# Depthwise taps on 32x32 tiles of TensorE: the two lanes interleaved tile by tile, in the order of columns

## The chip, the cores and the metric

The kernel runs on one NeuronCore of a Trainium2 chip. The metric is the device time of one execution in microseconds (us), and a kernel is judged by the median of its runs. TensorE (PE) multiplies and writes sums to PSUM; VectorE (DVE) and ScalarE (ACT) read PSUM and work on SBUF; GpSimd (POOL) and SyncE (SP) do little here but start DMAs.

## The reference, cut to what matters

The program is a net of four layers, x = x + layer(group_norm(x)), on x of 4 x 48 x 256 x 256 in f32. Layers 0 and 3 are feed-forward blocks with a spectral weight and a depthwise 3x3 convolution; layers 1 and 2 are line-by-line recurrences. Only layer 3 is touched by the change:

```python
y = jnp.einsum('oc,bchw->bohw', w_in, x)             # 48 -> 288 channels
f = jnp.fft.rfft2(yp) * fft_mask[None]               # in patches of 8 x 8
yp = jnp.fft.irfft2(f, s=(P, P))
...
y = lax.conv_general_dilated(y, w_dw, (1, 1), ((1, 1), (1, 1)), feature_group_count=C2)   # 3 x 3, per channel
x1, x2 = jnp.split(y, 2, axis=1)                     # 144 and 144 channels
g = jax.nn.gelu(x1, approximate=False) * x2
return jnp.einsum('oc,bchw->bohw', w_out, g)         # 144 -> 48
```

The depthwise convolution is nine taps: each output pixel is the sum over nine shifted input pixels of that channel, each times one weight.

## The kernel before

Layer 3 goes over the images in pairs. Each pair is cut into strips of eight rows, and one more short "tail" strip at the end of each pair, so there are 2 x 33 steps. In each step the strip is normalised (`normed`), turned and carried to the spectral basis (`turned`, `waves`, L1006 and L1021), multiplied by w_in and the mask (`spectrum`, `spectrum_rest`, L1040 to L1056) and carried back to pixels (`pixels`, `pixels_rest`, L1087 to L1113). The pixels stand in five tiles `zt`: a0 and a1 (the first 128 channels of x1 and of x2, first image), b0 and b1 (the same of the second image), and m (the 16 channels that are left, of both images).

**The taps.** A depthwise tap is a matmul with a diagonal 32 x 32 weight (`diag`): 32 channels (a block k of 32 partitions, a row block of the array) go to 32 partitions of PSUM (a column block j of the array). A matmul covers two image rows, 512 pixels; j counts the four pairs of rows of a strip. So block k and pair j name one of the sixteen 32 x 32 tiles of the array. `taps` (L1117) does a0, a1 and m in this way. `lower_taps` (L1130) does the lower half of the strip for b0 and b1, with the four column blocks made of two halves x two pairs of rows. The upper half of b is done by VectorE (`begin`, L1172, with L1183), one tap at a time from the list `due`.

**The two lanes.** A unit (`unit`, L1248) is one tile of PSUM sums, `pd`, of two banks: lane 0 has blocks 0 and 1, lane 1 has blocks 2 and 3. When its nine taps are done, the unit ends with the evacuation: `curve` (ScalarE Gelu, L1160), `gate` (VectorE product, L1166), or `lower_gate` (ScalarE L1149, then VectorE L1150). `together` (L1272) runs one unit of each lane side by side and is called a round here. A generator gives a whole tap of its lane at each step, so TensorE's queue holds, tap after tap, the eight matmuls of lane 0 and then the eight of lane 1. Within a lane the order is: for each column block, its two row blocks. Because m takes four blocks for both images, the lists of units are staggered: over two steps there are seven rounds, in which lane 0 does a0, a1, b, m, a0, a1, b and lane 1 does a0, a1, b, a0, a1, b, m.

**What sets the order.** On TensorE, VectorE and ScalarE the order is written out by hand (`manual_schedule`). The loop over steps (L1338) puts the spectral work of the next step and the pixels of this one between the rounds, and `store` (with `mixed`, L1197 to L1237) multiplies the last step's gated values by w_out, adds the input and writes the rows out. All sums of TensorE in layer 3 share one ring of four PSUM buffers (`ps_w`, tag "w"), each of two banks: a new tile waits until the tile four places before it has been evacuated. So the lane 0 `pd` of a round waits for one earlier tile and the lane 1 `pd` for the next one; the first two tiles after a round take the two other buffers, and the third one takes the buffer of lane 0.

Of the kernel before, what the change touches and what calls it, by code (L numbers as in the profile page):

```python
# [31 lines left out]
class Net:  # L32
# [848 lines left out]
    def layer3(self, x, scs):  # L881
# [9 lines left out]
        tail = lambda step: step[1] == H // RB  # L891
        odd = lambda step: steps.index(step) % 2
        with ExitStack() as st:
# [222 lines left out]

            def taps(step, g, half, blocks, pd):  # L1117
                for t in range(9):
                    for j in range(1 if tail(step) else 4):
                        n = 1 if tail(step) else R2  # L1120
                        for i, k in enumerate(blocks):
                            s = slice(32 * k, 32 * k + 32)
                            nc.tensor.matmul(  # L1123
                                pd[32 * j : 32 * j + 32, i, 0:n, :], diag[s, 2 if g == "m" else half, t, :],
                                zt[g][s, R2 * j + t // 3 : R2 * j + t // 3 + n, t % 3 : t % 3 + W],
                                start=(t == 0), stop=(t == 8),
                            )
                    yield True

            def lower_taps(step, blocks, pd):  # L1130


                for t in range(9):
                    for half in range(2):
                        for j in range(2, 4):
                            to = slice(64 * half + 32 * (j - 2), 64 * half + 32 * (j - 1))
                            for i, k in enumerate(blocks):
                                s = slice(32 * k, 32 * k + 32)
                                nc.tensor.matmul(  # L1139
                                    pd[to, i], diag[s, half, t, :],  # L1140
                                    zt[f"b{half}"][s, R2 * j + t // 3 : R2 * j + t // 3 + R2, t % 3 : t % 3 + W],
                                    start=(t == 0), stop=(t == 8),
                                )
                    yield True

            def lower_gate(k0, pd):
                gl = io.tile([128, 2, MM], F32, name="gl", tag="gl")
# [100 lines left out]
            def unit(l, step, img):  # L1248


                n, blocks = steps.index(step), (2 * l, 2 * l + 1)
                pd = None
                if img == "b":
                    if not tail(step):
                        pd = ps_w.tile([128, 2, R2, W], F32, name="pd", tag="w")
                        yield from lower_taps(step, blocks, pd)
                else:
                    pd = ps_w.tile([128, 2, R2, W], F32, name="pd", tag="w")
                    half = int(img[1]) if img[0] == "a" else 0
                    yield from taps(step, img, half, blocks, pd)  # L1260
                if img == "a0":
                    waiting[l] = curve(step, pd)
                    return
                assert n == 0 or steps[n - 1] in out
                if img == "a1":
                    gate(step, "a", 2 * l, waiting[l], pd)
                elif img == "m":
                    gate(step, img, 0, curve(step, pd[:, 0:1]), pd[:, 1:2])
                elif pd is not None:
                    lower_gate(2 * l, pd)  # L1270

            def together(k, aside=None):  # L1272


                going = [unit(l, *units[l][k]) for l in range(2)]
                for t in range(9):
                    for g in list(going):
                        if next(g, None) is None:
                            going.remove(g)
                    if t == 1 and aside is not None:  # L1280
                        aside()
                    if due and (t + 1) * 5 // 9 > t * 5 // 9:
                        due.pop(0)[1]()
                for g in going:
                    assert next(g, None) is None
# [51 lines left out]
            k = 0  # L1337
            for n, step in enumerate(steps):  # L1338
# [6 lines left out]
                if even:  # L1345
                    turn(n + 1, "AD")
                together(k, None if even else lambda: ready(n + 1))

                pixels(step, "a1", "DD")
# [6 lines left out]
                else:  # L1356
                    turn(n + 1, "AA")
                together(k + 1)

                upper(n, 1, "AA")  # L1360
# [3 lines left out]
                else:  # L1364
                    wave(n + 1, "AA")
                    spectra(n + 1, 0, slice(0, 2))
                together(k + 2)
                k += 3
                if not even:
# [118 lines left out]
```

## Time and profile before

| what | value |
|---|---|
| median of 3 runs | 13252.56 us (13247.61 to 13270.56) |
| the profiled execution, its own time | 13259.28 us |
| its span, first to last instruction | 13257.5 us |
| mean granted TensorE clock | 0.966 |
| layer 3's taps, first to the end of the program | 8690 to 13257 us |
| TensorE busy in the span | 12356.8 us (93%) |
| matmuls L1123 into sums from z_a, from z_m; L1139 | 37152, 9288; 18432 records |

How to read it: times in the profile are in us, those of single instructions in ns. PE is TensorE's matmuls and PEld its weight loads. A line of groups gives the source line, engine, operation, the tiles out<-in with their shapes, the number of instructions, then busy time and the mean time of one, and then the idle time of the engine just before them with what ended it. A line in order of time gives the start, the length from the first start to the last end, and the number of instructions that were merged into it; square brackets hold idle time and its releaser. Matmuls overlap on the array, so the length of one is much more than its share of the time.

### The profile page before, as it was taken

The page shows a single profiled execution, that of the slowest core. Times are in us where ns is not written, and L with a number is a line of the kernel's source. Part 1 is how long each engine was busy: PE and PEld are TensorE (multiplying, and loading weights), DVE is VectorE, ACT ScalarE, POOL GpSimd, SP SyncE. Part 2 cuts the span into 40 slices and gives each one's busy share as a digit, 9 for nine tenths or more (in the row PEclk, how much of TensorE's full clock was granted, in tenths as well). Part 3 has the DMA queues.
Part 4 walks back from the last instruction along what each step waited for, and adds up shares of the span by engine and source line. Part 5 has one row for each costly group of instructions (what it writes and reads, how often), then busy time and mean ns, then how long its engine had stood idle before and what let it go on. Part 6 is the DMA issues. An engine that isn't in the chain of part 4 may idle for free.

```text
span 13257.5 us, 432328 instructions
## 1 busy us (share of the span) xinstructions
PE 12356.8 (93%) x203336; PEld 8155.9 (62%) x203336; DVE 7417.3 (56%) x10766; ACT 3602.9 (27%) x4043; POOL 1336.7 (10%) x977
## 2 busy tenths in 40 slices
PE   2999999998999899999998999989999999999999
PEld 1333333335777677767776777666666666666666
DVE  6777777773333334653333336556666666666666
ACT  1444444442223100002232000033333333333333
POOL 0011011010000002530000015400000000000000
PEclk9999999998999999999999999889999999999999
DMA  7222222225755876987657769711111111111110
GB/s 171 59 55 57 55 57 59 52 54 101 153 134 153 172 153 147 229 177 152 136 153 165 157 135 220 179 31 27 23 27 27 24 27 23 27 27 23 27 27 20
DMA packets 1170374, 1225.00 MB, mean 92 GB/s; under 512 B 1027669, under 2 KB 1031757, under 8 KB 1107725
## 3 DMA queue, kind: packets, MB, share of 16 engines
q1 hardware_dynamic: 1070476, 649.55, 25.6%
q0 software_dynamic: 87488, 445.55, 11.6%
q10 hardware_dynamic: 10624, 102.24, 4.4%
q8 instruction: 1592, 26.08, 0.9%
q14 instruction: 194, 1.58, 0.0%
HBM read 699.76 MB, written 497.42 MB: 90 GB/s over the span
## 4 chain that ended last, share of the span: by engine, by line
PE 88%; ACT 4%; issue 3%; DVE 3%; DMA 2%; SPq 0%; POOL 0%; DVEq 0%; ACTq 0%; POOLq 0%
PE acc L661 40%; PE pd L1123 12%; PE pd L308 9%; PE pd L1139 5%; PE pz L1040 4%; PE pp L1087 4%; PE po L1215 2%; PE ph L285 2%; PE pz L1053 2%; DMA gx<-in_x 1%; PE ph L277 1%; PE py L382 1%; PE po L452 1%; PE py L389 1%; PE po L1205 1%
## 5 line engine op out<-in xcount | busy, mean ns | idle before, releaser
L661 PE MATMUL acc<-line,w_down 96*96 96x256 f32 x12240 | 2692.9, 382 | 53.0 <-ACT line L731 31.8
L661 PEld LDWEIGHTS acc<-line,w_down 96*96 96x96 f32 x12240 | 2008.1, 164 | 730.1 <-DVE line L740 34.1
L1123 PE MATMUL pd<-z_a,diag 32*32 32x512 f32 x37152 | 1626.2, 599 | 57.8 <-issue 49.4
L308 PE MATMUL pd<-main,diag 32*32 32x512 f32 x36864 | 1427.2, 621 | 81.4 <-issue 77.3
L661 PE MATMUL acc<-line,w_right 96*96 96x256 f32 x6120 | 1341.0, 380 | 81.8 <-DVE line L811 59.8
L661 PE MATMUL acc<-line,w_left 96*96 96x256 f32 x6120 | 1362.9, 384 | 31.2 <-DVE line L852 31.2
L1183 DVE SCALAR_TENSOR_TENSOR acc<-z_b,wd,acc 128x1024 f32<-128x1024 f32 (+1 forms) x1056 | 1326.5, 1259 | 34.4 <-ACT acc L1178 7.1
L345 DVE SCALAR_TENSOR_TENSOR acc<-rest,wd,acc 128x1024 f32<-128x1024 f32 x1024 | 1257.8, 1292 | 126.9 <-ACT acc L339 126.6
L1123 PEld LDWEIGHTS pd<-z_a,diag 32*32 32x32 f32 x37152 | 890.6, 103 | 604.0 <-issue 232.9
L661 PEld LDWEIGHTS acc<-line,w_right 96*96 96x96 f32 x6120 | 1000.1, 164 | 412.6 <-DVE line L811 61.1
L661 PEld LDWEIGHTS acc<-line,w_left 96*96 96x96 f32 x6120 | 1007.9, 165 | 377.5 <-DVE line L852 47.1
L308 PEld LDWEIGHTS pd<-main,diag 32*32 32x32 f32 x36864 | 505.2, 105 | 798.1 <-issue 684.4
L1139 PE MATMUL pd<-z_b,diag 32*32 32x512 f32 x18432 | 973.7, 642 | 0.5 <-ACT z_b L999 0.5
L740 DVE TENSOR_TENSOR line<-acc,in 96x256 f32<-96x256 f32 x1020 | 428.9, 421 | 961.6 <-PE acc L661 948.7
L814 DVE SCALAR_TENSOR_TENSOR line<-acc,b_right,in 96x256 f32<-96x256 f32 x1020 | 489.4, 480 | 836.4 <-PE acc L661 836.4
L775 DVE SCALAR_TENSOR_TENSOR line<-acc,b_down,in 96x256 f32<-96x256 f32 x992 | 475.9, 480 | 811.5 <-PE acc L661 810.6
L120 ACT ACTIVATE nrm<-nrm 96x2 f32<-96x2 f32 (+2 forms) x5 | 1.0, 204 | 2989.4 <-DVE nrm L119 2989.4
L852 DVE SCALAR_TENSOR_TENSOR line<-acc,b_left,in 96x256 f32<-96x256 f32 x992 | 475.8, 480 | 564.2 <-PE acc L661 564.2
L862 POOL TENSOR_TENSOR blk<-blk,line 96x1024 f32<-96x1024 f32 x248 | 705.2, 2873 | 644.3 <-DVE line L852 644.3
L1043 DVE TENSOR_TENSOR z<-pz,mask 128x1024 f32<-128x1024 f32 x512 | 601.2, 1219 | 276.2 <-PE pz L1040 273.7
L782 ACT COPY blk<-line 96x1024 f32<-96x1024 f32 (+2 forms) x264 | 480.0, 1891 | 978.0 <-DVE line L775 816.0
L1087 PEld LDWEIGHTS pp<-c_inv,z 64*64 64x64 f32 x32768 | 515.9, 135 | 228.8 <-issue 204.6
(167 smaller groups left out, 13065.8 us busy)
## 6 DMA issues: line engine op xcount, KB each, us to landing
blk<-x ACTq DMA_DIRECT2D x64, 1536.0 KB, 19.3
in<-x SPq DMA_DIRECT2D x248, 384.0 KB, 11.0
dn<-line POOLq DMA_DIRECT2D x124, 768.0 KB, 9.6
rt<-line POOLq DMA_DIRECT2D x124, 768.0 KB, 9.6
in<-rt SPq DMA_DIRECT2D x124, 768.0 KB, 12.6
in<-dn SPq DMA_DIRECT2D x120, 768.0 KB, 5.8
in<-up SPq DMA_DIRECT2D x240, 384.0 KB, 9.3
up<-blk POOLq DMA_DIRECT2D x56, 1536.0 KB, 14.3
```

The lines of the kernel that those rows point to most:

```text
L308: nc.tensor.matmul(pd[32 * j : 32 * j + 32, i], diag[s, t, :], z[s, R2 * j + t // 3 : R2 * j + t // 3 + R2, t % 3 : t % 3 + W], start=(t = ...
L345: nc.vector.scalar_tensor_tensor(to, at(t, r), wd[:, 1, t : t + 1], to, ALU.mult, ALU.add)
L661: self.nc.tensor.matmul(acc, w[:, t, :], carry[:, :, t : t + m], start=(t == 0), stop=(t == 2))
L782: nc.scalar.copy(blk[:, :, e, lo:hi, k // 2 : k // 2 + RH], inner(ln[:, e::2])[..., lo:hi].rearrange("p h i w -> p i w h"),)
L814: nc.vector.scalar_tensor_tensor(blocks(inner(line)), blocks(acc), br, new, ALU.add, ALU.add)
L862: (nc.vector if w0 == 0 else nc.gpsimd).tensor_tensor(part, part, inner(ln[:, f::2])[..., lo:hi].rearrange("p w i h -> p i h w"), ALU.add)
L1040: nc.tensor.matmul(pz[:, b, q, :], xf[s, q0 + q, :], wi[s, NM * k : NM * k + NM], start=True, stop=True)
L1043: nc.vector.tensor_tensor(zs[k][:, q0 : q0 + 4].rearrange("p q b c -> p b q c"), pz, mask[:, :, :, NM * k : NM * k + NM].to_broadcast([128 ...
L1087: nc.tensor.matmul(pp[64 * c : 64 * c + 64, l, q, :], z[f, q0 + q, b, 64 * c : 64 * c + 64], self.inv1[f, :], start=True, stop=True,)
L1123: nc.tensor.matmul(pd[32 * j : 32 * j + 32, i, 0:n, :], diag[s, 2 if g == "m" else half, t, :], zt[g][s, R2 * j + t // 3 : R2 * j + t // 3 ...
L1139: nc.tensor.matmul(pd[to, i], diag[s, half, t, :], zt[f"b{half}"][s, R2 * j + t // 3 : R2 * j + t // 3 + R2, t % 3 : t % 3 + W], start=(t ...
L1183: nc.vector.scalar_tensor_tensor(acc, at(t), wd[:, half, t : t + 1], acc, ALU.mult, ALU.add)
```

## The change

In `taps` the generator now stops after each column block j, not after each tap: it has given two matmuls (one for each of the lane's two row blocks). In `lower_taps` it stops after each pair of matmuls too. `together` steps both lanes four times per tap. TensorE's queue so holds, in each tap: column block 0 of lane 0 (row blocks 0 and 1), column block 0 of lane 1 (row blocks 2 and 3), column block 1 of lane 0, and so on: the sixteen tiles in the order of columns. In a tail step only column block 0 has work, and the other three stops are empty. What happens once per tap beside it (`aside` at t == 1, a VectorE tap from `due`) stays where it was. The weights, the sums, the buffers and their number, and the instructions of the other engines are the same.

```diff
             def taps(step, g, half, blocks, pd):
                 for t in range(9):
-                    for j in range(1 if tail(step) else 4):
+                    for j in range(4):
                         n = 1 if tail(step) else R2
-                        for i, k in enumerate(blocks):
+                        for i, k in enumerate(blocks) if j == 0 or not tail(step) else ():
                             s = slice(32 * k, 32 * k + 32)
                             nc.tensor.matmul(
                                 pd[32 * j : 32 * j + 32, i, 0:n, :], diag[s, 2 if g == "m" else half, t, :],
                                 zt[g][s, R2 * j + t // 3 : R2 * j + t // 3 + n, t % 3 : t % 3 + W],
                                 start=(t == 0), stop=(t == 8),
                             )
-                    yield True
+                        yield True
...
             def lower_taps(step, blocks, pd):
...
                                     start=(t == 0), stop=(t == 8),
                                 )
-                    yield True
+                            yield True
...
                 going = [unit(l, *units[l][k]) for l in range(2)]
                 for t in range(9):
-                    for g in list(going):
-                        if next(g, None) is None:
-                            going.remove(g)
+                    for _ in range(4):
+                        for g in list(going):
+                            if next(g, None) is None:
+                                going.remove(g)
                     if t == 1 and aside is not None:
                         aside()
```

## The prediction

> **What bounds the kernel now.** I read the page first, then the windows of the stage that the change touches, then single rounds of it in order of time.
>
> ```profile
> span 13257.5 us, 432328 instructions
> PE 12356.8 (93%) x203336; PEld 8155.9 (62%) x203336; DVE 7417.3 (56%) x10766; ACT 3602.9 (27%) x4043; POOL 1336.7 (10%) x977
> ...
> PE 88%; ACT 4%; issue 3%; DVE 3%; DMA 2%; SPq 0%; POOL 0%; DVEq 0%; ACTq 0%; POOLq 0%
> PE acc L661 40%; PE pd L1123 12%; PE pd L308 9%; PE pd L1139 5%; PE pz L1040 4%; PE pp L1087 4%; PE po L1215 2%; PE ph L285 2%; PE pz L1053 2%; DMA gx<-in_x 1%; PE ph L277 1%; PE py L382 1%; PE po L452 1%; PE py L389 1%; PE po L1205 1%
> ...
> L1123 PE MATMUL pd<-z_a,diag 32*32 32x512 f32 x37152 | 1626.2, 599 | 57.8 <-issue 49.4
> L1139 PE MATMUL pd<-z_b,diag 32*32 32x512 f32 x18432 | 973.7, 642 | 0.5 <-ACT z_b L999 0.5
> ```
>
> TensorE is the path, and the lines that change (L1123, L1139) hold 17% of it, all in layer 3. From the first L1123 to the end:
>
> ```profile
> 8690.00:13257.00 4567.00, 4376.90 (x127017) 3056.65 (x127014) 2934.61 (x3068) 1589.31 (x2325) 5.69 (x15) 0.97 0.12 25
> ```
>
> TensorE is busy 4376.9 of 4567.0 us. Every f32 matmul of the program is two records, a first and a second pass, each with its weight load: 288 records for the 9 x 16 matmuls of a round. So a gain has to come from a denser round, and a loss from a round that starts or ends later. One round, lane 0 under L1123 and lane 1 under L1139:
>
> ```profile
> 10495.76 0.66 PE L1123 MATMUL pd<-z_a,diag 32*32 32x512 f32 x8
> 10495.81 0.66 PE L1139 MATMUL pd<-z_b,diag 32*32 32x512 f32 x8
> 10496.21 0.63 PE L1123 MATMUL pd<-z_a,diag 32*32 32x512 f32 x8
> 10496.27 0.63 PE L1139 MATMUL pd<-z_b,diag 32*32 32x512 f32 x8
> 10496.64 0.90 PE L1123 MATMUL pd<-z_a,diag 32*32 32x512 f32 x8
> 10496.95 0.72 PE L1139 MATMUL pd<-z_b,diag 32*32 32x512 f32 x8
> ```
>
> All sixteen first passes begin within 0.1 us, then all sixteen second passes: already in the old order sixteen tiles run at once. The first tap takes 0.857 us (two passes of 0.429). The second starts at 10496.64 with one matmul alone; the next weight load comes at 10496.831. That is 0.031 us after the first matmul's second pass has ended (10496.213, and 0.587 long). In a round at half clock the same load comes at 8729.318, where that pass began at 8728.231 and took 1.056: again 0.031. So the load of matmul n+17 waits until matmul n has wholly ended. Later taps confirm 17, not 16: the stalled load moves one matmul earlier in each tap, through both lanes and all columns. A matmul's turn is 0.027 (load) + 0.429 (first pass) + 0.587 (second, to its end) + 0.030 = 1.073 us for 17 matmuls. The last of 144, number 143 = 8 x 17 + 7, ends at 8 x 1.073 + 7 x 0.017 + 1.043 = 9.75 us; 93 of the 220 rounds that I could separate last 9.75.
>
> [...]
>
> **The change, part by part.** No matmul, wait or buffer is added or removed, and no other engine's queue changes. Inside each tap lane 1's matmuls move from places 8-15 to places 2, 3, 6, 7, 10, 11, 14, 15.
>
> (1) *The steady rate.* Each tile still returns after 16 matmuls, and the distance of 17 does not ask which tile. I cost it at 0; bounds with rivals C and D.
>
> (2) *The start.* Lane 1's first matmul waits for its own PSUM buffer. In the old order eight matmuls of lane 0 stand ahead of it and run meanwhile; in the new one two do, and six are queued behind the waiting one.
>
> ```profile
> 8882.38 4.62 DVE L1043 TENSOR_TENSOR z<-pz,mask 128x1024 f32<-128x1024 f32 x4
> ...
> 8885.98 1.09 PE L1123 MATMUL pd<-z_m,diag 32*32 32x512 f32 x16
> ...
> 8887.05 0.16 PEld L1123 LDWEIGHTS pd<-z_a,diag 32*32 32x32 f32 x13 [0.89 <-DVE z L1043]
> ...
> 8895.77 1.75 ACT L1160 ACTIVATE gl<-pd 128x512 f32<-128x512 f32 x2 [2.30 <-PE pd L1123]
> ```
>
> Lane 0 starts at 8885.98 (16 records: its eight matmuls alone), lane 1 at 8887.05, one VectorE operation later: d = 1.07. Such rounds last d + 9.42 (10.48 at d = 1.07, 10.04 at d = 0.62). With only two matmuls ahead a round lasts what a whole one does, from d on, less 2 x 0.017: d + 9.71. Loss 0.29 us. Lane 1 starts over 0.11 us late in 86 of 220 rounds. 28 of them lie on the d + 9.42 line: 28 x 0.29 = 8.1 us. Nearly all others stall a second time further on, and a long second stall lets both lanes catch up, so I take half: 52 x 0.145 = 7.5. The six others have d under 0.33 and lose some 0.15, halved too: 0.4. Sum: **16 us**. Bounds: 8 (those on the line alone) and 24 (all).
>
> (3) *The end.* In the old order lane 0's sums are complete ahead of lane 1's, in most rounds by 0.33 us; in the new one its last matmul is two places before the last, 0.03 ahead. ScalarE's or VectorE's evacuation of lane 0 starts 0.3 later, and lane 1's, queued behind it, as well. Who waits for that?
>
> ```profile
> 10587.59 1.93 ACT L1149 ACTIVATE gl<-pd 64x1024 f32<-64x1024 f32 x2 [17.15 <-PE pd L1139]
> ...
> 10588.64 2.37 DVE L1150 TENSOR_TENSOR g_b<-gl,pd 64x1024 f32<-64x1024 f32 x2 [4.79 <-ACT gl L1149]
> ...
> 10589.92 0.97 PEld L1040 LDWEIGHTS pz<-wi,xf 48*128 48x128 f32 x16 [0.24 <-DVE g_b L1150]
> ```
>
> After rounds that hold L1139's sums in both lanes, or in lane 0 with m beside it, TensorE's next PSUM buffer is released by L1150: about 27 and 25 times in the trace. A shift of 0.22 in the first kind (lanes end 0.24-0.33 apart) and 0.29 in the second: 27 x 0.22 + 25 x 0.29 = **13 us**. After a0 and a1 rounds two L1087 groups (2.1 us each at most) come ahead of the first buffer that lane 0 held, and they cover 0.3; if that cover were gone, another 160 x 0.3 = 48 would follow. I add **4** for rounds that lack it. Bounds: 0 and 24, half of that uncovered sum, since TensorE reaches such a buffer with about 0.3-0.8 us to spare.
>
> Sum: 0 + 16 + 13 + 4 = **+33 us**. The profiled execution took 13259.28 us (span 13257.5 and 1.8 around it) and lies 6.7 above the median of 13252.56; a difference carries over, so 13252.6 + 33, rounded to **13285**. Measurement can tell about 0.2% (26.5 us) from no change.
>
> **The rivals.** A (forecast, chance 0.57): 13285, its own range 13265 to 13325, from the lower bounds 8 + 6 to the upper 24 + 13 + 24 with a little room; four fifths of it lies above 13279.
> B (0.19): the waits are absorbed, because VectorE moves on while TensorE is late and the next wait is shorter by as much: 13250 to 13265. For it: only 28 late rounds show the clean form. Against it: the evacuations wait for TensorE themselves (L1149's 17.15 us idle ended by pd), so they shift along.
> C (0.17): faster. With lanes in turns, neighbours sit in four row blocks, and if it is the row block that holds the next weight loads back, they would enter earlier. At the full rate every tap takes the first one's 0.857 where it now takes 16/17 of 1.073 = 1.010: a round of 8.0, 1.73 saved, x 224 rounds = -388, 12865. It decides as soon as the second tap's loads come before 10496.83 in the place shown. Against it: the stall moves through all rows and columns without a change of rate. Of the 0.17, 0.06 is a small form, a gain of up to 25 at the start of rounds whose second z tile is late.
> D (0.07): four neighbours in one column of the array hinder each other, one more stream (0.214) in each of eight taps: +1.71 x 224 = +384, 13637. Against it: sixteen passes run at once today.
>
> **How the numbers follow.** Slower by over 0.2%: 0.46 of A and D's 0.07, 0.53. Within: 0.11 of A and B's 0.19, 0.30. Faster: 0.17. A, B and C's small form are 0.82, so the range is 13225 to 13340; C's full form and D stay out.
>
> **What would show it.** Right: rounds without a late lane still 9.75, first taps 0.857, loads 17 apart; late rounds at d + 9.71; lane 0's last signal 0.03 before lane 1's; longer waits on L1150. Wrong: a round under 9.7 (C), one over 10 with no wait in it (D), or late rounds still at d + 9.42.

## The result, and the profile after

| what | before | after |
|---|---|---|
| median of the runs, us | 13259.64 of 12 (13230.36 to 13276.54) | 13291.53 of 12 (13277.11 to 13307.46) |
| ratio, 95% interval | | 1.0026 (1.0018 to 1.0034) |
| span of the profiled execution, us | 13257.5 | 13297.6 |
| mean granted TensorE clock | 0.966 | 0.965 |
| layer 3, first tap to the end, us | 4567.1 | 4598.9 |
| rounds that last no more than 9.76 us: number of 220, median us | 93, 9.748 | 88, 9.748 |
| lane 0's last signal ahead of lane 1's, median us | 0.333 | 0.034 |

The changed kernel is 0.26% slower: 34 us, from 24 to 45. Here and below the microseconds of a ratio are (ratio - 1) x 13260. The last three rows are worked out from the records of each trace. The two traces have spans 40.1 us apart; 31.8 of that lies in layer 3, and 8.4 ahead of its first tap, in layers that the change doesn't touch. So a single trace differs from another by some microseconds without a cause in the change. From the page after, the head and the group of L1123:

```profile
span 13297.6 us, 432329 instructions
...
PE 12381.2 (93%) x203336; PEld 8151.0 (61%) x203336; DVE 7417.5 (56%) x10766; ACT 3597.9 (27%) x4043; POOL 1335.2 (10%) x977
...
L1123 PE MATMUL pd<-z_a,diag 32*32 32x512 f32 x37152 | 1659.2, 598 | 60.3 <-issue 51.3
```

No engine has more to do, and a matmul lasts as long as before (598 ns, was 599). Busy time rose by 24.4 us on TensorE although the work is the same, which fits rounds in which fewer matmuls overlap, since TensorE counts as busy when only a few tiles run: in the place shown below, from 8898.00 to 8898.49, it is busy for 0.49 of 0.49 us with four records. So the busy share says nothing here, and single rounds must be read. A round after, in order of time:

```profile
10664.83 0.62 PE L1123 MATMUL pd<-z_a,diag 32*32 32x512 f32 x2
10664.85 0.11 PEld L1139 LDWEIGHTS pd<-z_b,diag 32*32 32x32 f32 x2
10664.85 0.62 PE L1139 MATMUL pd<-z_b,diag 32*32 32x512 f32 x2
...
10665.72 0.80 PE L1123 MATMUL pd<-z_a,diag 32*32 32x512 f32 x2
10665.72 0.29 PEld L1123 LDWEIGHTS pd<-z_a,diag 32*32 32x32 f32 x2 [0.33 <-issue]
10665.92 0.10 PEld L1139 LDWEIGHTS pd<-z_b,diag 32*32 32x32 f32 x1
```

The lanes take turns two by two, as written. The second tap starts 0.89 after the first one, as in the round shown of before (10496.64 - 10495.76 = 0.88), and again with one matmul alone: the next load (the second one in the line of 0.29) comes at 10665.906, 0.19 later. That is 0.031 after the round's first matmul has ended its second pass (10665.288, and 0.587 long), so the distance of 17 is there in the new order too. The pace within a round has not changed. Now the place where a round of b in both lanes is followed by one of m (lane 0) and a (lane 1):

```profile
8889.06 1.93 ACT L1149 ACTIVATE gl<-pd 64x1024 f32<-64x1024 f32 x2 [15.74 <-PE pd L1139]
8890.10 2.37 DVE L1150 TENSOR_TENSOR g_b<-gl,pd 64x1024 f32<-64x1024 f32 x2 [4.48 <-ACT gl L1149]
...
8893.82 4.62 DVE L1043 TENSOR_TENSOR z<-pz,mask 128x1024 f32<-128x1024 f32 x4
...
8897.78 1.05 PE L1123 MATMUL pd<-z_m,diag 32*32 32x512 f32 x4
...
8898.49 0.11 PEld L1123 LDWEIGHTS pd<-z_a,diag 32*32 32x32 f32 x2 [0.57 <-DVE z L1043]
```

Only four records of lane 0 (two matmuls) run at 8897.78 while lane 1 waits for L1043, where sixteen did before; six matmuls of lane 0 stand behind the waiting one, and the first of them starts at 8898.506, after it. And lane 1's buffer is the end of a chain on VectorE: L1150, L999, four times L1043. In all 31 such places, with the end of TensorE's last matmul of the b round as zero (medians, us):

| from the records | before | after |
|---|---|---|
| L1150 starts | 0.850 | 1.051 |
| the last L1043 ends | 9.187 | 9.386 |
| lane 1 of the next round starts | 9.242 | 9.440 |
| from there to that round's end | 9.416 | 9.714 |

The chain itself is as long as before (8.34 us); it starts 0.20 later, because lane 0's sums are complete 0.20 later, and lane 1's start moves with it. Then the round takes 0.30 longer from lane 1's start. That is the end's loss and the start's loss, one after the other: 31 x (0.20 + 0.30) = 15.5 us.

One more thing had moved. TensorE's waits ahead of L1040, from the profile's answer on that line after:

```profile
  ACT z_a L999: 24.0, 59
  DVE g_b L1150: 18.1, 50
```

Before, L1150 had 7.9 us in 39 waits, and L999 under z_a none from ScalarE. The semaphores in the records show why: once in two steps (31 times) the second z tile after a round of b in both lanes takes the buffer that L999 copies out, and the third one takes lane 1's; before it was the other way round. The kernel's text asks for four buffers in a ring, but a tile doesn't get the one of four places before it everywhere; which one it gets is the same in all 31 places of a trace, and with the new order of the taps it is another one here. The prediction took the order of the buffers as fixed. So a third suspect came up beside start and end: the exchanged buffers.

### The profile page after: what moved, and what is told of

Its sections match the earlier page's. It is cut to its first block, busy times and chain, and to the rows that moved or that the text cites. A ratio compares the mean times of both kernels' runs of the same rounds, so it can differ in the third digit from the quotient of the medians.

```text
span 13297.6 us, 432329 instructions
## 1 busy us (share of the span) xinstructions
PE 12381.2 (93%) x203336; PEld 8151.0 (61%) x203336; DVE 7417.5 (56%) x10766; ACT 3597.9 (27%) x4043; POOL 1335.2 (10%) x977
## 4 chain that ended last, share of the span: by engine, by line
PE 87%; ACT 5%; issue 3%; DVE 2%; DMA 2%; SPq 0%; POOL 0%; DVEq 0%; ACTq 0%; POOLq 0%
PE acc L661 40%; PE pd L1123 12%; PE pd L308 9%; PE pd L1139 5%; PE pz L1040 4%; PE pp L1087 3%; PE po L1215 2%; PE pz L1053 2%; PE ph L285 2%; DMA gx<-in_x 1%; PE ph L277 1%; PE py L382 1%; PE po L452 1%; PE py L389 1%; PE po L1205 1%
## 5 line engine op out<-in xcount | busy, mean ns | idle before, releaser
L1123 PE MATMUL pd<-z_a,diag 32*32 32x512 f32 x37152 | 1659.2, 598 | 60.3 <-issue 51.3
L1123 PEld LDWEIGHTS pd<-z_a,diag 32*32 32x32 f32 x37152 | 850.5, 103 | 587.6 <-issue 242.5
L1043 DVE TENSOR_TENSOR z<-pz,mask 128x1024 f32<-128x1024 f32 x512 | 600.7, 1219 | 272.0 <-PE pz L1040 269.1
L1123 PE MATMUL pd<-z_m,diag 32*32 32x512 f32 x9288 | 653.6, 596 | 0.0
```

Of the source, the lines that this page charges most:

```text
L1043: nc.vector.tensor_tensor(zs[k][:, q0 : q0 + 4].rearrange("p q b c -> p b q c"), pz, mask[:, :, :, NM * k : NM * k + NM].to_broadcast([128 ...
L1123: nc.tensor.matmul(pd[32 * j : 32 * j + 32, i, 0:n, :], diag[s, 2 if g == "m" else half, t, :], zt[g][s, R2 * j + t // 3 : R2 * j + t // 3 ...
```

## The experiments

All ratios are to the kernel before on the same chip; the first line repeats the result. "Turns" are the lanes alternating inside a tap, and "exchanged" means the pair of buffers just described.

| kernel | turns in taps | buffers | ratio (95%) | us |
|---|---|---|---|---|
| after | 0 to 8 | exchanged | 1.0026 (1.0018 to 1.0034) | 34 |
| first tap by lanes | 1 to 8 | exchanged | 1.0017 (1.0008 to 1.0025) | 23 |
| last tap by lanes | 0 to 7 | as before | 1.0011 (1.0004 to 1.0019) | 15 |
| both by lanes | 1 to 7 | as before | 1.0007 (0.9999 to 1.0016) | 9 |
| only first tap in turns | 0 | as before | 1.0008 (0.9998 to 1.0018) | 11 |
| only last tap in turns | 8 | exchanged | 1.0011 (1.0004 to 1.0018) | 15 |
| lane 1 first | none | exchanged | 1.0015 (1.0006 to 1.0023) | 20 |
| columns, old buffers | 0 to 8 | as before | 1.0025 (1.0018 to 1.0033) | 33 |
| lanes, exchanged buffers | none | exchanged | 1.0003 (0.9993 to 1.0013), twice | 4 |
| row blocks inside a lane | none | as before | 1.0005 (0.9998 to 1.0013) | 7 |

### Undoing the first tap, the last, or both

In `together`, with `t == 0`, with `t == 8`, and with `t in (0, 8)`:

```diff
-                    for _ in range(4):
-                        for g in list(going):
-                            if next(g, None) is None:
-                                going.remove(g)
+                    turns = ((g, k) for g in list(going) for k in range(4)) if t == 0 else (
+                        (g, k) for k in range(4) for g in list(going)
+                    )
+                    for g, _ in turns:
+                        if g in going and next(g, None) is None:
+                            going.remove(g)
```

First tap by lanes. 

> The order of columns, but tap 0 again lane after lane. Theory 'start and end' (the loss sits where lane 1's first matmul waits and where lane 0's last one stands; the order between is free): the start is mended, the end is not. Late rounds lie on d + 9.49 to 9.52 (before d + 9.42, in the changed kernel d + 9.65), lane 0's last signal still 0.03 us ahead of lane 1's, L1150's waits as long as in the changed kernel; the time is 14 to 22 us above before. Rival 'middle' (seven taps in lane turns cost something in themselves): late rounds stay near d + 9.65 and the time is 25 to 30 above before. Rival 'start alone' (the whole loss is at the start): within 5 us of before.

Measured: +23 us (11 to 33). From lane 1's start to the end of the m and a round it takes 9.52 us (after 9.714, before 9.416), as expected; L1150 still starts at 1.051 and lane 1 at 9.439. The time alone doesn't exclude the rival "middle"; the round does.

Last tap by lanes. 

> The order of columns, but tap 8 lane after lane. Theory 'start and end': the end is mostly mended, the start is not. Lane 0's last signal stands 0.23 us ahead of lane 1's (before 0.33, changed 0.03), the waits of L1087's and L1040's first loads on L1150 come back towards 0.22 and 0.29 us, late rounds stay at d + 9.65; the time is 12 to 22 us above before. Rival 'middle': 25 to 30 above before. Rival 'end alone': within 8 us of before.

Measured: +15 us (5 to 25). Lane 0's last signal is 0.233 ahead, L1150 starts at 0.851 and lane 1 at 9.240, as before; the round still takes 9.720 from there. TensorE's first loads of L1087 that waited for L1150 fell from 11.4 to 5.6 us.

Both by lanes. 

> The order of columns in taps 1 to 7 only; taps 0 and 8 lane after lane. Theory 'start and end': both mended, late rounds on d + 9.5, lane 0's last signal 0.23 us ahead; the time is 2 to 10 us above before. Rival 'middle': still 22 to 30 us above before, as most of the new order is still there.

Measured: +9 us (-1 to 21). The middle is out as the carrier of the loss: with seven of nine taps still in the new order the time is 25 us below the changed kernel's. The 9 us that are left are not clear of zero.

### Lane 1 first, without any turns

The order of before, with lane 1's tap ahead of lane 0's:

```diff
                 going = [unit(l, *units[l][k]) for l in range(2)]
+                for g in going:
+                    next(g)
                 for t in range(9):
-                    for g in list(going):
+                    for g in going[::-1]:
```

(`unit` stops once more, after its buffer is taken.)

> The order of before, a whole tap of a lane at a time and no turns within a tap, but in each tap lane 1's eight matmuls stand ahead of lane 0's. The buffers are taken in the old order. So lane 1's late buffer now holds up everything, and lane 0, whose buffer is needed first after the round, ends last. Theory 'start and end': the loss is that of the changed kernel or a little more, though no column order is in it: late rounds at d + 9.7, lane 1's last signal ahead of lane 0's by 0.3 us, the waits on L1150 (and on L1166) longer; 20 to 45 us above before. Rival 'middle' (the order of columns costs): within 8 us of before.

Measured: +20 us (8 to 30), but half of the expectation fell. The waits show that lane 1, which now writes first, got the buffer that is free first, and lane 0 the late one. So the late lane again has eight matmuls ahead of it, and the round takes 9.422 from its start, as before. What is left is the end (and the exchanged buffers, tried below): the sums that ScalarE takes first are complete last. L1150 starts at 1.084, and TensorE's loads waited for it:

```profile
  PEld pz L1040: 12.3, 28
  PEld pp L1087: 12.1, 27
```

That is more than in the changed kernel (10.8 and 11.4), with no column order in the kernel at all. The end costs something without any turns.

### The two parts alone

The mirrors of the first two kernels: `t != 0` and `t != 8` in the same lines.

> The mirror of the kernel with tap 0 lane after lane: the lanes in turns in tap 0 alone, taps 1 to 8 lane after lane. The start's loss without the middle and the end; the buffers are handed out as before. Theory 'two places': late rounds on d + 9.65, lane 0's last signal about 0.33 us ahead of lane 1's in whole rounds, the waits on L1150 as before; the time is 8 to 16 us above before, and the stretches from a round of b in both lanes to the end of the second round after it hold it. Rival 'middle' (only turns in the middle taps cost): within 4 us of before.

Measured: +11 us (-3 to 24). The interval doesn't exclude zero; the rounds decide. L1150 starts at 0.846 and lane 1 at 9.229, as before, and the round takes 9.715 from there, all of the loss that the changed kernel has at the start. Its waits on L1150 are those of before (7.9 us in 39 there):

```profile
  PEld pz L1040: 7.8, 40
```

> The mirror of the kernel with tap 8 lane after lane: the lanes in turns in tap 8 alone. The end's loss without the start and the middle; the one pair of buffers is exchanged as in the changed kernel. Theory 'two places': late rounds on d + 9.42 to 9.5, lane 0's last signal 0.03 us ahead, the waits on L1150 as long as in the changed kernel; the time is 12 to 24 us above before. Rival 'middle': within 4 us of before.

Measured: +15 us (5 to 24). L1150 at 1.052, lane 1 at 9.437, and 9.416 from there: the end's loss without the start's. The two parts add up to 26 us of the 34; the intervals leave room for the whole.

### The exchanged buffers

The four buffers are given out by hand, from a list of slots; where `flips` is set, the next tile takes the second one in the list. For the changed kernel with the old buffers:

```diff
-            ps_w = pool("ps3w", 4, space=PSUM)
+            ring, slots, flips = pool("ps3w", 1, space=PSUM), list("0123"), []
+
+            class ps_w:
+                @staticmethod
+                def tile(shape, dtype, name, tag):
+                    slots.append(slots.pop(len(flips)))
+                    flips.clear()
+                    return ring.tile(shape, dtype, name=name, tag="w" + slots[-1])
...
+                if g == "a1" and not odd(step) and not tail(step):
+                    flips.append(1)
```

The last two lines, in `pixels`, give an exchange that the kernel before has as well. The other kernel, the old order of taps with the exchanged pair, adds a second one ahead of the second z tile.

> The changed kernel with its order of columns, but the PSUM buffers are handed out in the order that the kernel before uses. The changed kernel takes one pair the other way round, once in two steps: the second z tile after a round of b in both lanes takes the buffer that ScalarE's L999 copies out, not the one that L1150 releases, and L999 ends 0.36 us later. Theory 'three places' (start of late rounds, later end of lane 0, swapped buffers): the swap's share goes, some 31 x 0.36 = 11 us; the time is 18 to 27 us above before, and that z tile waits for L1150 again. Rival 'two places' (the swap is hidden, since the engine waits elsewhere for as long): 30 to 36 above before, as the changed kernel.

> The kernel before, its taps lane after lane, with the changed kernel's order of buffers alone: the second and third z tile after a round of b in both lanes exchange their buffers. Theory 'three places': 7 to 14 us above before, all of it in the gap ahead of that z tile, now ended by ScalarE's L999. Rival 'two places': within 4 us of before.

> The kernel before with the exchanged pair of buffers alone, once more, since the first measurement (1.0003, 0.9993 to 1.0013) does not tell 11 us from nothing. 'Three places': 1.0006 to 1.0010. 'Two places' (the late z tile only shortens the wait of lane 1 in the next round, which VectorE's L1043 ends): 0.9998 to 1.0004.

Measured: +33 us (24 to 44) without the exchange, +4 (-9 to 17) with nothing but the exchange, and once more 1.0003 (0.9993 to 1.0013). That favours "two places", but the intervals alone don't exclude the 11 us of "three places". The wait is real: in the first trace of the exchange alone the gap ahead of that z tile's first weight load grew from 3.7 to 13.1 us in sum over the 31 places. Where did 9 us go? From the first trace of that kernel (its lines stand 12 lower: L1135 is L1123, L1053 is L1043):

```profile
8896.67 1.09 PE L1135 MATMUL pd<-z_m,diag 32*32 32x512 f32 x16
...
8897.37 0.16 PEld L1135 LDWEIGHTS pd<-z_a,diag 32*32 32x32 f32 x13 [0.53 <-DVE z L1053]
```

Lane 1 starts 0.70 us after lane 0 here, where it was 1.07 in before's trace. TensorE comes to the round 0.35 us later (8.529 after the end of the b round, before 8.175), and lane 1 at 9.233 as before (9.242): L1043 on VectorE sets it. Up to there the new wait only shortened the next one. So "two places" stands, by the rounds more than by the ratios.

### Other orders of the tiles

In `taps` and `lower_taps` the loops over row blocks and column blocks are exchanged, the lanes left alone:

```diff
-                    for j in range(1 if tail(step) else 4):
+                    for i, k in enumerate(blocks):
...
-                        for i, k in enumerate(blocks):
+                        for j in range(1 if tail(step) else 4):
```

> The kernel before, but inside a lane's tap the row block is the outer loop and the column block the inner one: four matmuls of one row block follow each other. The lanes, the buffers and the ends of the lanes stay. Theory (only 17 matmuls in flight count, whichever tiles they are on): within 4 us of before, whole rounds 9.75 us, first tap 0.857. Rival 'row blocks hold the weight loads back': whole rounds over 10 us and the time some 60 us or more above before, or under 9.5 and as much below.

Measured: +7 us (-3 to 17), whole rounds 9.754, and the second tap starts 0.88 after the first one. Which tile follows which inside a lane is of no account in these rounds.

### Half of the stream

> Leaves out half of the pixels in taps 1 to 7: those matmuls stream one image row (256) instead of two. In the kernel before otherwise. Theory 'window of 17' (a matmul's whole stay, from its load to its full end, is what a place in the window costs): a pass of 256 takes half of 0.429, its fixed tail stays (0.587 - 0.429 = 0.158), so a turn is 0.027 + 0.214 + 0.373 + 0.030 = 0.644 us for 17 matmuls instead of 1.073; a round without a late lane lasts about 6.7 us instead of 9.75. With a window of 16 it would be 6.9; if the streams alone set the rate, 7 x 0.43 + 2 x 0.86 and the tail, 4.9 to 5.1. The program is 500 to 670 us shorter than before.

The matmuls of taps 1 to 7 take `0 : 1` of the two rows, in operand and sums, so half of their pixels are left out. This is a single run. Measured: the shortest round lasts 6.77 us; the sum of the expectation, with taps 0 and 8 at full length, gives 6.74 for a distance of 17 and 6.88 for 16. But only ten of the 220 rounds are under 7.2, and the program took 13044.46 us, 219 below the median of before and not 500 to 670. Most rounds have one or two pauses of 0.5 to 1.2 us more, put down to "issue", for which the profile shows no releaser (idle ahead of L1123's z_a matmuls 218.3 us, was 57.8), and the stretches between rounds grew: in the traces the 220 rounds take 351 us less than before in sum, and what lies between them 139 us more. So the shortest round fits a distance of 17; what the pauses are stays open.

## Why the prediction was right, point by point

**The forecast.** 13285 was said and 13291.53 came; +33 and +34 (24 to 45). The mechanism was the one named: a late start and a later end, with nothing in between. That the sizes agree to 1 us is luck. Of the 34 us only 15.5 are read from single rounds, 7 of the 33 arrive nowhere, and less certain stretches make up the rest.

**(1) The steady rate, 0: right.** Whole rounds 9.748 before and after, and 9.754 with the row blocks exchanged. Rivals C and D, which decide at this place, fall: no round is under 9.7 (the shortest is 9.747 before and 9.746 after), and whole rounds have not become longer. (D's 0.214 a tap was an estimate, half of the 0.429 that a pass took.) C's small form, a gain where the second z tile is late, falls with the rounds of m and a, which lost.

**(2) The start, 16: right in size and place, with another make-up.** 0.29 for each clean late round was predicted, and it is 9.714 - 9.416 = 0.30. It holds in the 31 rounds of m and a: 9.3 us (8.1 were counted as clean, 21 of these and 7 of a and a). The half taken for rounds that stall a second time is right only on average. The rounds of a and a that follow m and a are all late, 31 of 31. From the end of the m and a round to theirs it took 21.92 us before (mean), 22.32 after and 22.20 with the turns in the first tap alone, so that this stretch would bear nearly all of it: 31 x 0.28 = 9 us by the latter. But the exchange alone, which has no turns, has 22.14 here in its first trace and 21.98 in its second, so these 9 us aren't clear of the spread. The late rounds a step further (a and a after a and a) bear nothing: 24.19 before, 24.15 after. Start in sum, about 18, of which 9.3 are shown round by round; by the ratios it is 11, both for the first tap undone (34 - 23) and for the first tap alone.

**(3) The end, 13 and 4 more: half right.** The first kind, 27 x 0.22 = 6, is 31 x 0.20 = 6.2, but on another path than the one named. The prediction let TensorE's wait at L1040 stand for it; the kernels with exchanged buffers show that waits of TensorE at L1040 can grow by 9 us while lane 1 starts as before, since its L1043 ends last. The loss passes along VectorE's queue (L1150 starts 0.20 later, the last L1043 ends 0.20 later). The second kind, 25 x 0.29 = 7, **failed**. TensorE's weight loads that waited for L1150 (us in all, times), before:

```profile
  PEld pz L1040: 7.9, 39
```

and after:

```profile
  PEld pp L1087: 11.4, 26
  PEld pz L1040: 10.8, 25
```

The wait grew as foreseen: after the rounds of b and m the load of L1087 that waits for L1150 starts 2.03 us after the round's end before and 2.33 after (medians of 31; its gap 0.144 and 0.443). Yet nothing of it arrives. The next group starts at 3.29 before and 3.26 after (medians; the means, 3.41 and 3.51, keep a third of the shift), because an unexplained pause in between became shorter in most places. From the end of these rounds to the end of the next it takes 17.09 and 16.97 (means). For the 4 us of uncovered rounds no run shows anything.

**What is left.** The two stretches that hold the loss, from the end of a b round through m and a to the end of the next a round, are 31 x (0.489 + 0.406) = 27.7 us longer in the trace after. The first stretch ends with the m and a round, the second with the a round. All kernels by the same sum:

| kernel, against before | both stretches, us | first stretch, us |
|---|---|---|
| after | 27.7 | 15.2 |
| columns, old buffers | 28.1 | 14.6 |
| first tap by lanes | 17.0 | 12.4 |
| last tap by lanes | 14.7 | 9.0 |
| both by lanes | 4.8 | 5.6 |
| only first tap in turns | 16.3 | 7.5 |
| only last tap in turns | 10.4 | 8.4 |
| lane 1 first | 13.2 | 11.1 |
| exchange alone, two traces | 9.4 and 2.1 | 2.5 and 0.3 |
| row blocks inside a lane | 1.8 | 2.3 |

So one trace is good to some 7 us in such a sum, and the order of the kernels is that of their ratios only roughly: only the first tap in turns stands above lane 1 first here, and below it by the ratio. The first stretch is the steadier one, and its 15.2 us agree with the 15.5 of end and start in the result. The rest of the 34 us, some 6, is not placed. The layer's other stretches don't stand still either: in the trace after, the one from a and b to b and m is 13.0 us longer. The one from a and a to b and b is 9.7 us shorter, and it is 8 to 24 us shorter in the other kernels' traces too, so there the trace of before is a long one. A possible reason for the former: between the rounds of a and b and of b and m TensorE is 10.7 us away in some places and 12.3 in others, in every kernel (the long one 13 of 31 times before, 22 after), and those counts differ from trace to trace of one kernel (17 and 12 with the exchange alone).

**Rival B** (the waits are absorbed, 0.19) was wrong for the sum and right for two of its parts: the exchanged buffers and the second kind of L1150's waits. It is the remark that was made for it: here a wait was worth what the next wait didn't give back (9 us more ahead of the z tile, lane 1's start at 9.233 and 9.242).

No order of the taps beat the kernel before. In the old order the late lane has eight matmuls of work ahead of it and the lane whose sums are needed first is complete first; each departure shows in the rounds (0.30 us after the late lane's start, 0.20 us at L1150), though by the time alone the first tap in turns isn't clear of zero.

## What to carry to other kernels

Where two lanes of work share one engine's queue, ask of a new order what stands behind the first instruction that may have to wait (here six matmuls behind a weight load that waited 0.57 us), and which lane's last instruction is awaited first; in between, the order was free here (whole rounds 9.748 us in both). Price the shift at its far end: follow it along the engine that it delays to the next wait that TensorE can't avoid, since a wait on the way that grows may only shorten the next, as the 9 us of the exchanged buffers did. And look whether a changed order also changes which buffer each tile gets: the list of what each wait waits for shows it, the text of the kernel doesn't.

## What of the hardware was not expected

A growth of 9 us in a wait of TensorE, in a program that keeps TensorE busy for 93% of its span (before: 12356.8 of 13257.5 us), left the start of lane 1 where it was (9.233 us, before 9.242), because the wait behind it was VectorE's; the time moved by 4 us (-9 to 17). With matmuls of half the length the shortest round still fits a distance of 17 (6.77 us measured, 6.74 by the sum, 6.88 with 16), but most rounds then meet pauses of 0.5 to 1.2 us for which nothing in the profile stands.
